# Spreading the queries over the edges: three bf16 products a chunk in place of one fp32 product

## The chip, the core and the metric

One core of a Trainium2 chip runs the whole program. Five engines work beside each other, each taking its own instructions in order: TensorE (PE; its weight loads are listed apart as PEld), VectorE (DVE), ScalarE (ACT), GpSimd (POOL) and SyncE (SP, which only issues transfers). The metric is the device time of one execution in microseconds (us), and lower is better. Three runs of the kernel before took 3375.17, 3377.44 and 3378.18 us; the median is 3377.44 us.

## The reference, cut to what matters

The program is a network of four graph layers with an expert layer behind each, over 3125 nodes of 256 features and 53125 edges. Only the first layer, the attention over the edges, is touched. There, each edge takes the dot product, per head, of its source's key and its destination's query:

```python
q = (nfeat @ Wq.T).reshape(n, HEADS, HEAD_DIM) / SCALING     # SCALING = 32 ** -0.5
k = (nfeat @ Wk.T).reshape(n, HEADS, HEAD_DIM)
v = (nfeat @ Wv.T).reshape(n, HEADS, HEAD_DIM)
attn = jnp.einsum('ehd,ehd->eh', k[src], q[dst])
attn = attn + attn_bias
m = jax.ops.segment_max(attn, dst, num_segments=n)
a = jnp.exp(attn - m[dst])
s = jax.ops.segment_sum(a, dst, num_segments=n)
a = a / s[dst]
out = jax.ops.segment_sum(v[src] * a[:, :, None], dst, num_segments=n)
return out.reshape(n, FEAT) @ Wo.T
```

The edges are sorted by destination. The change is in how `q[dst]` is made.

## The kernel before

The nodes are cut into 25 tiles of 125 (`P`, `T`). The edges that end in a tile lie in a window of 18 chunks (`WC`) of 128 edges. A chunk's rows of keys and values (2 KB an edge) are gathered from memory by POOL, one indirect transfer a chunk (`gathered`, L1656), six chunks to a tile `kv`, of which seven buffers exist.

`q[dst]` is a product with a one-hot matrix. The tile `oht` holds, for each of the 125 destinations (partitions) and each of the window's 2304 edges, whether the edge ends there. It arrives as a transfer of edge destinations to all partitions (`asked`, L1808), and a comparison with the partition's number on DVE turns it into ones and zeros in bf16, in place (`one_hot_turned`, L1834). Before the change ACT then casts it into fp32, in three tiles `oht_f` of six chunks (L1838). The queries of the tile (`queries`, L1825) are a product of the normalised rows with Wq on PE, scaled on ACT into an fp32 tile `q`.

`logits` (L1841) runs three times a tile, over six chunks each: for two chunks at a time PE multiplies `oht_f` with `q` into PSUM (L1849; the tile `qx`, two buffers), and DVE multiplies the keys by it in place (L1851). A reduction over each head's 32 features follows (L1852). `sums_of` (L1856) adds the edges' bias, takes the exponential on ACT, and sums it per destination by 18 small bf16 products (L1864), which DVE copies into `sums` (L1866). `weights_of` (L1868) makes the final weights, again with 18 small products, now with the bf16 `oht` (L1876). `weighted` (L1883) multiplies the values by them on DVE (L1886), casts the other one-hots into fp32 on ACT (`oh_f`, L1891), and adds up on PE (L1893; the tile `acc`). When `acc` has read a `kv` tile, POOL may fill it anew. `normed`, `normed_turned` and `projected` end the tile with an addition to `x` (L1917).

The loop at L1924 is a software pipeline: in iteration t the logits of tile t, the weights and sums of rows of tile t-1, and the one-hots and queries of tile t+1 are made; `beside` puts parts of the first expert layer in between (their products have the helper's line L266), and `windows.next()` parts of a preparation of a later stage, which sends a small table to memory and fetches it again (L2028 to L2040). A scheduler then orders each engine's instructions; SP's and POOL's queues keep the order in which they are built.

Of the kernel before, what the change touches and what calls it, by code (L numbers as in the profile page):

```python
# [10 lines left out]
F32 = mybir.dt.float32  # L11
F32R = mybir.dt.float32r
I32 = mybir.dt.int32
BF16 = mybir.dt.bfloat16
AF = mybir.ActivationFunctionType
# [7 lines left out]
N, D = 3125, 256  # L23
P, T = 125, 25
# [11 lines left out]
H, HD = 8, 32  # L36
# [12 lines left out]
WC, PC = 18, 6  # L49
# [21 lines left out]
def gnn_ffn_kernel(ctx: ExitStack, tc: tile.TileContext, a, out: bass.AP):  # L71
    nc = tc.nc
# [187 lines left out]
    def product(ps, terms, bias=None):  # L260

        last = len(terms) - 1
        if bias is not None:
            nc.tensor.matmul(ps, ones_h[:bias.shape[0], :ps.shape[0]], bias, start=True, stop=False)
        for i, (l, r) in enumerate(terms):
            nc.tensor.matmul(ps, l, r, start=(bias is None and i == 0), stop=(i == last))  # L266
# [1360 lines left out]
    def attention(windows, experts):  # L1627
# [11 lines left out]
        with ExitStack() as es:  # L1639
# [5 lines left out]
            sums = big.tile([P, T, H], F32, name="sums")  # L1645
# [10 lines left out]
            def gathered(at):  # L1656


                kv = rows_tile()
                for c in range(PC):  # L1660
                    got = nc.gpsimd.indirect_dma_start(  # L1661
                        out=kv[:, c, KO:], out_offset=None, in_=kv_d,
                        in_offset=bass.IndirectOffsetOnAxis(ap=src_i[:, at + c:at + c + 1], axis=0))
                    if len(under_way) > 4:
                        tc.add_manual_dep(got.ins, under_way[-5].ins.name, data_dep, reason="in turn")
                    under_way.append(got)
                nc.vector.memset(kv[:, :, KO - 1:KO], 1.0)
                return kv
# [3 lines left out]
            pool = setup.enter_context(tc.tile_pool(name="att_in", bufs=2, reuse_waits="tile"))  # L1672
# [128 lines left out]
            pool = es.enter_context(tc.tile_pool(name="att_s", bufs=2, reuse_waits="tile"))  # L1801
# [23 lines left out]
            def queries(s):  # L1825

                ps = psum.tile([P, D], F32, name="sm")
                product(ps, [(s.lt[:, k, :], wq[:, k, :]) for k in range(2)])
                s.q = pool.tile([P, D], F32, name="q")
                nc.scalar.activation(s.q, ps, AF.Copy, scale=float(HD) ** 0.5)  # L1830

            def one_hot_turned(s):
                v = s.oht.rearrange("d c e -> d (c e)")
                nc.vector.tensor_scalar(v, v, pcol[:P], None, ALU.is_equal)  # L1834
                s.oht_f = []
                for c0 in range(0, WC, PC):
                    s.oht_f.append(pool.tile([P, PC, 128], F32, name="oht_f", bufs=3))
                    nc.scalar.copy(s.oht_f[-1], s.oht[:, c0:c0 + PC, :])  # L1838
                s.l = pool.tile([128, WC, H], F32, name="l")

            def logits(s, p):  # L1841

                if p == len(s.kv):
                    s.kv.append(gathered(s.t * WC + p * PC))
                kv = s.kv[p]
                for c0 in range(0, PC, 2):
                    ps = psum.tile([128, 2, D], F32, name="qx", bufs=2)
                    for c in range(2):
                        nc.tensor.matmul(ps[:, c, :], s.oht_f[p][:, c0 + c, :], s.q, start=True, stop=True)  # L1849
                    k_ = kv[:, c0:c0 + 2, KO:VO]  # L1850
                    nc.vector.tensor_mul(k_, k_, ps)  # L1851
                nc.vector.tensor_reduce(  # L1852
                    s.l[:, p * PC:(p + 1) * PC, :],
                    kv[:, :, KO:VO].rearrange("p c (h d) -> p c h d", h=H), AX.X, ALU.add)

            def sums_of(s):  # L1856

                nc.vector.scalar_tensor_tensor(s.l, s.l, 640.0, s.eb.rearrange("p h c -> p c h"),
                                               ALU.min, ALU.add)
                el = pool.tile([128, WC, H], BF16, name="el")  # L1860
                nc.scalar.activation(el, s.l, AF.Exp, scale=1.0 / 8.0)
                ps = psum.tile([P, 512], F32, name="sm")
                for c in range(WC):
                    nc.tensor.matmul(ps[:, :H], s.oh[:, c, :], el[:, c, :], start=(c == 0),  # L1864
                                     stop=(c == WC - 1))
                nc.vector.tensor_copy(sums[:, s.t, :], ps[:, :H])  # L1866

            def weights_of(s):  # L1868

# [49 lines left out]
            now, before = asked(0), None  # L1919
            one_hot(now)  # L1920
            one_hot_turned(now)
            queries(now)
            more = experts()
            for t in range(T + 1):  # L1924
# [4 lines left out]
                if now:  # L1929
                    logits(now, 0)  # L1930
# [10 lines left out]
                if after:  # L1941
                    one_hot_turned(after)
                    queries(after)
                beside()
                if now:
                    logits(now, 1)
# [4 lines left out]
                if now:  # L1951
                    logits(now, 2)
# [3 lines left out]
                if now:  # L1956
                    sums_of(now)
# [572 lines left out]
```

## Time and profile before

The profiled execution took 3376.49 us; its span, from the first to the last instruction, is 3374.6 us. Shares of the span and counts, and the same for the stage of the attention, 121 to 870 us:

| engine | whole span, busy us | share | stage, busy us | share of 749 us |
|---|---|---|---|---|
| PE | 3116.4 | 92% | 692.8 | 92% |
| PEld | 2442.6 | 72% | 548.2 | 73% |
| DVE | 1704.7 | 51% | 571.7 | 76% |
| ACT | 1064.6 | 32% | 251.6 | 34% |
| POOL | 691.1 | 20% | 460.8 | 62% |

The costliest groups of the stage beside those that the change touches are, by line: L1893 on PE (the sums of rows, 213.9 us), L1852 on DVE (the reduction, 130.9 us), L1886 on DVE (the values times the weights, 127.6 us), and POOL's gathers (L1661, 451.7 us). The queries' own step on ACT, L1830, takes 9.4 us in 25 instructions, and the comparison L1834 on DVE 20.5 us in 25.

Two things help in reading these numbers. A matmul's end is modelled, and the next one starts before it, so a "mean ns of one" is longer than the time that it takes from PE; the distance between starts is that time. And a product of fp32 operands appears as two records.

### The profile page before, as it was taken

The page shows a single profiled execution, that of the slowest core. Times are in us where ns is not written, and L with a number is a line of the kernel's source. Part 1 is how long each engine was busy: PE and PEld are TensorE (multiplying, and loading weights), DVE is VectorE, ACT ScalarE, POOL GpSimd, SP SyncE. Part 2 cuts the span into 40 slices and gives each one's busy share as a digit, 9 for nine tenths or more (in the row PEclk, how much of TensorE's full clock was granted, in tenths as well). Part 3 has the DMA queues.
Part 4 walks back from the last instruction along what each step waited for, and adds up shares of the span by engine and source line. Part 5 has one row for each costly group of instructions (what it writes and reads, how often), then busy time and mean ns, then how long its engine had stood idle before and what let it go on. Part 6 is the DMA issues. An engine that isn't in the chain of part 4 may idle for free.

```text
span 3374.6 us, 43621 instructions
## 1 busy us (share of the span) xinstructions
PE 3116.4 (92%) x15687; PEld 2442.6 (72%) x15687; DVE 1704.7 (51%) x4763; ACT 1064.6 (32%) x2074; POOL 691.1 (20%) x639
## 2 busy tenths in 40 slices
PE   6698999999888999999996999979999999999898
PEld 2477777777677798898885888868755555579666
DVE  6587778777686434244673122166511111355662
ACT  1233333333355323232331222234323323332120
POOL 1676666655000000000234333200000000000000
PEclk9799999999899999999997999989999999999897
DMA  5876666655256634343445666564200000053001
GB/s 164 256 218 175 191 185 167 200 164 162 84 182 221 153 97 122 95 118 92 105 108 161 185 186 177 138 153 102 53 19 10 19 10 10 7 128 102 16 1 39
DMA packets 257578, 402.66 MB, mean 119 GB/s; under 512 B 42704, under 2 KB 202319, under 8 KB 257348
## 3 DMA queue, kind: packets, MB, share of 16 engines
q1 hardware_dynamic: 188465, 241.20, 25.6%
q0 software_dynamic: 54064, 141.25, 15.8%
q10 hardware_dynamic: 14819, 17.27, 2.0%
q8 instruction: 128, 2.10, 0.3%
q14 instruction: 102, 0.84, 0.1%
HBM read 328.87 MB, written 70.70 MB: 118 GB/s over the span
## 4 chain that ended last, share of the span: by engine, by line
PE 67%; DVE 5%; DMA 3%; issue 3%; ACT 2%; POOL 0%; SPq 0%; ACTq 0%; POOLq 0%; DVEq 0%
PE agg L2233 21%; PE po L266 19%; PE hid_ps L266 15%; PE tr L266 2%; PE row L266 1%; PE tok L1536 1%; PE acc L1893 1%; PE tr L2321 1%; PE tr L250 1%; DVE hr L282 1%; DMA kv<-kv_d,src_w 1%; PE qx L1849 1%; ACT h L1376 1%; DVE hc L282 0%; PE s L266 0%
## 5 line engine op out<-in xcount | busy, mean ns | idle before, releaser
L2233 PE MATMUL agg<-cnt_f,hp 125*128 125x500 f32 (+1 forms) x3500 | 733.7, 369 | 23.3 <-ACT hp L2174 22.9
L2233 PEld LDWEIGHTS agg<-cnt_f,hp 125*128 125x128 f32 x3500 | 635.9, 189 | 104.5 <-ACT hp L2174 24.0
L1661 POOL DMA_INDIRECT kv<-kv_d,src_w x450 | 467.4, 1039 | 233.5 <-issue 109.5
L2211 ACT CAST cnt_f<-blk 125x500 fp32r<-125x500 bf16 (+1 forms) x435 | 245.5, 565 | 519.5 <-PE agg L2233 489.7
L2211 DVE CAST cnt_f<-blk 125x500 fp32r<-125x500 bf16 (+1 forms) x440 | 184.9, 422 | 266.6 <-PE agg L2233 221.7
L1382 DVE SCALAR_TENSOR_TENSOR x<-po,gall,x 125x256 f32<-125x256 f32 x200 | 93.8, 484 | 417.5 <-PE po L266 416.9
L1376 ACT ACTIVATE h<-hid_ps,shift,scale 128x500 f32<-128x500 f32 (+1 forms) x224 | 161.7, 722 | 376.2 <-PE hid_ps L266 375.6
L1849 PE MATMUL qx<-q,oht_f 125*128 125x256 f32 x900 | 240.3, 399 | 14.6 <-DVE kv L1851 11.6
L1893 PE MATMUL acc<-kv,oh_f 128*125 128x265 f32 x900 | 219.2, 399 | 1.9 <-DVE kv L1886 1.9
L1849 PEld LDWEIGHTS qx<-q,oht_f 125*128 125x128 f32 x900 | 170.2, 197 | 50.3 <-DVE kv L1851 20.8
L266 PE MATMUL po<-wslot,h 128*125 128x256 f32 x800 | 203.0, 386 | 0.1
L1893 PEld LDWEIGHTS acc<-kv,oh_f 128*125 128x125 f32 x900 | 173.5, 194 | 37.0 <-DVE kv L1886 4.1
L266 PEld LDWEIGHTS po<-wslot,h 128*125 128x125 f32 x800 | 145.0, 187 | 75.2 <-ACT h L1376 27.0
L266 PE MATMUL hid_ps<-h,wslot 128*128 128x500 f32 (+1 forms) x448 | 193.6, 555 | 4.1 <-ACT h L1376 0.6
L1072 POOL DMA_INDIRECT xs_d<-r_l,pos x50 | 60.1, 1203 | 646.6 <-DVE r_l L1068 568.3
L266 PE MATMUL hid_ps<-xe,wslot 128*128 128x256 f32 x832 | 187.4, 383 | 1.8 <-DVE xe L1214 1.8
L1225 ACT ACTIVATE hid<-hid_ps,wslot 128x256 f32<-128x256 f32 x208 | 98.3, 474 | 287.2 <-PE hid_ps L266 287.2
L266 PE MATMUL hid_ps<-v_rows,wslot 128*128 128x500 f32 (+1 forms) x448 | 186.8, 537 | 0.0
L266 PE MATMUL po<-wslot,hid 128*128 128x256 f32 x832 | 184.5, 378 | 0.0
L266 PEld LDWEIGHTS hid_ps<-xe,wslot 128*128 128x128 f32 x832 | 150.8, 191 | 33.2 <-ACT hid L1225 3.6
L266 PEld LDWEIGHTS po<-wslot,hid 128*128 128x128 f32 x832 | 155.7, 189 | 21.8
L1851 DVE TENSOR_TENSOR kv<-kv,qx 128x512 f32<-128x512 f32 x225 | 150.7, 680 | 32.6 <-PE qx L1849 29.9
(509 smaller groups left out, 4535.4 us busy)
## 6 DMA issues: line engine op xcount, KB each, us to landing
wslot<-in_ex_W SPq DMA_DIRECT2D x52, 1024.0 KB
blk<-an_d SPq DMA_DIRECT2D x60, 546.9 KB
blk<-at_d SPq DMA_DIRECT2D x40, 546.9 KB
blk<-an_d SPq DMA_DIRECT2D x45, 410.2 KB
at_d<-ab SPq DMA_DIRECT2D x25, 683.6 KB
an_d<-an SPq DMA_DIRECT2D x25, 683.6 KB
oht<-turned_d SPq DMA_DIRECT2D x25, 504.0 KB
blk<-at_d SPq DMA_DIRECT2D x30, 410.2 KB
```

What stands on the lines that cost most here:

```text
L250: nc.tensor.transpose(ps[:, i * P:(i + 1) * P], src[:, i, k * 128:(k + 1) * 128], ident[:P, :P])
L266: nc.tensor.matmul(ps, l, r, start=(bias is None and i == 0), stop=(i == last))
L1072: st = nc.gpsimd.indirect_dma_start(out=xs_d, in_=l2[:, i, :].bitcast(I32), in_offset=None, out_offset=bass.IndirectOffsetOnAxis(ap=self.p ...
L1225: nc.scalar.activation(hid[:, m, :], ps[:, :BLK], AF.Gelu, bias=c[:, 4 + m:5 + m])
L1376: nc.scalar.activation(dst[:, m, :c], ps[:, :c], AF.Relu, bias=shift[:, l, col:col + 1], scale=scale[:, l, col:col + 1])
L1382: nc.vector.scalar_tensor_tensor(x[:, t0 + i, :], po, gating.all[:, t0 + i, e:e + 1], x[:, t0 + i, :], ALU.mult, ALU.add)
L1661: got = nc.gpsimd.indirect_dma_start(out=kv[:, c, KO:], out_offset=None, in_=kv_d, in_offset=bass.IndirectOffsetOnAxis(ap=src_i[:, at + c: ...
L1849: nc.tensor.matmul(ps[:, c, :], s.oht_f[p][:, c0 + c, :], s.q, start=True, stop=True)
L1851: nc.vector.tensor_mul(k_, k_, ps)
L1893: nc.tensor.matmul(s.acc[:, :D + H + 1], of[:, c, :], kv[:, c, AO:VO], start=(p == 0 and c == 0), stop=(p == 2 and c == PC - 1))
L2211: to(f[:, :n, :], part[0][:, :n, m % MB, :])
L2233: nc.tensor.matmul(ps[f][:, :c], hp[:, m, k, f * 128:(f + 1) * 128], got[:, :c], start=(m == 0 and k == 0), stop=(m == T - 1 and k == 1))
```

## The change

`queries` now splits the fp32 queries into three bf16 parts, whose sum carries them: the first part is the rounded query, the second the rounded rest, the third what is then left. `logits` multiplies each chunk's one-hots by the three parts in turn, adding up in PSUM, and takes the bf16 one-hots `oht` as the comparison leaves them. The casts into `oht_f` are gone, and so are its three buffers. The copy of the sums moves from DVE to ACT.

```diff
             def queries(s):
                 ps = psum.tile([P, D], F32, name="sm")
                 product(ps, [(s.lt[:, k, :], wq[:, k, :]) for k in range(2)])
-                s.q = pool.tile([P, D], F32, name="q")
-                nc.scalar.activation(s.q, ps, AF.Copy, scale=float(HD) ** 0.5)
+                s.q = pool.tile([P, 3, D], BF16, name="q_t")
+                q = pool.tile([P, D], F32, name="q", bufs=1)
+                nc.scalar.activation(q, ps, AF.Copy, scale=float(HD) ** 0.5)
+                nc.scalar.copy(s.q[:, 0, :], q)
+                nc.vector.tensor_sub(q, q, s.q[:, 0, :])
+                nc.scalar.copy(s.q[:, 1, :], q)
+                nc.vector.tensor_sub(s.q[:, 2, :], q, s.q[:, 1, :])

             def one_hot_turned(s):
                 v = s.oht.rearrange("d c e -> d (c e)")
                 nc.vector.tensor_scalar(v, v, pcol[:P], None, ALU.is_equal)
-                s.oht_f = []
-                for c0 in range(0, WC, PC):
-                    s.oht_f.append(pool.tile([P, PC, 128], F32, name="oht_f", bufs=3))
-                    nc.scalar.copy(s.oht_f[-1], s.oht[:, c0:c0 + PC, :])
                 s.l = pool.tile([128, WC, H], F32, name="l")
...
                     for c in range(2):
-                        nc.tensor.matmul(ps[:, c, :], s.oht_f[p][:, c0 + c, :], s.q, start=True, stop=True)
+                        for k in range(3):
+                            nc.tensor.matmul(ps[:, c, :], s.oht[:, p * PC + c0 + c, :], s.q[:, k, :],
+                                             start=(k == 0), stop=(k == 2))
...
-                nc.vector.tensor_copy(sums[:, s.t, :], ps[:, :H])
+                nc.scalar.copy(sums[:, s.t, :], ps[:, :H])
```

## The prediction

> **What bounds the kernel now.** I read the page first, then only the attention stage, 121 to 870 us: nothing else of the program is touched (the instructions after the loop stand in the same order in both programs).
>
> Groups of that stage by line, operation and shape (count | busy us, mean ns | idle before it and who ended it):
>
> ```profile
> L1849 PE MATMUL qx<-q,oht_f 125*128 125x256 f32 x900 | 240.3, 399 | 14.6 <-DVE kv L1851 11.6 <-DVE g_rank L716 1.3 <-DVE l L1879 0.5
> L1851 DVE TENSOR_TENSOR kv<-kv,qx 128x512 f32<-128x512 f32 x225 | 150.7, 680 | 32.6 <-PE qx L1849 29.9 <-DMA kv<-kv_d,src_w 1.8
> ...
> L1838 ACT CAST oht_f<-oht 125x768 f32<-125x768 bf16 x75 | 60.6, 829 | 59.6 <-PE qx L1849 26.9 <-DVE oht L1834 26.0 <-DVE kv L1667 5.9
> ```
>
> There are 18 chunks in each of 25 tiles, 450 products, but 900 records: one fp32 product is two passes over its 256 columns. ACT's casts cost 60.6 us, and ACT waits for others, not others for it: of the waits that end in a cast, PE's own are 2.1 us in all.
>
> The busy time of stretches (PE, PEld, DVE, ACT, POOL, each with its count; then the granted clock, the DMA share and GB/s) shows who sets the pace. I cut at each tile's last addition to x (L1917) and then over the stage:
>
> ```profile
> 642.00:676.40 34.40, 33.71 (x181) 26.72 (x180) 26.74 (x61) 11.00 (x23) 26.77 (x26) 1.00 0.77 219
> 676.40:700.90 24.50, 22.43 (x131) 17.74 (x129) 22.42 (x48) 9.99 (x20) 10.08 (x11) 1.00 0.48 139
> ...
> 270.20:308.40 38.20, 31.33 (x158) 23.83 (x157) 20.01 (x42) 11.19 (x23) 26.75 (x27) 0.87 0.80 189
> 121.00:870.00 749.00, 692.82 (x3734) 548.19 (x3735) 571.74 (x1155) 251.57 (x513) 460.79 (x441) 0.96 0.65 181
> ```
>
> Three kinds of tile. With the expert work beside it, a tile is PE's: 33.7 of 34.4 us busy, DVE waiting. Without, it is as much DVE's: 22.4 of 24.5 us on both. And some stand still for a transfer: in 270 to 308 PE is busy 31.3 of 38.2 us. Of the 24 tiles so cut, 13 have PE busy 95% or more; of the other 11, three early ones have POOL's gathers without a pause, about six stand for a transfer, the rest are DVE's.
>
> **PE, the main term.** The price of a product is the distance between starts, since ends are modelled. In the timeline (start, us, what):
>
> ```profile
> 617.82 1.89 PE L1849 MATMUL qx<-q,oht_f 125*128 125x256 f32 x8
> ...
> 625.03 0.59 PE L1876 MATMUL sm<-m,oht 125*128 125x8 bf16 x18
> ...
> 1056.94 0.56 PE L2121 MATMUL bt<-ident_h,ab 125*125 125x125 bf16 x7 [0.19 <-DVE an L2124]
> ...
> 3198.18 0.38 PE L264 MATMUL row<-bs,ones_h 128*125 128x512 bf16 x1
> 3198.40 1.02 PE L266 MATMUL row<-w_slices,lt 128*125 128x512 f32 x2
> ```
>
> An fp32 record of 256 columns takes (1.89 - 0.38)/7 = 216 ns, 0.38 being the modelled length of one, so a chunk takes 432 ns. No bf16 product of 256 columns is in the trace, but both neighbours are: 125 columns take (0.56 - 0.22)/6 = 56 ns, and 512 take 220 ns until the next start. On that line, 0.424 ns a column, 256 columns are 111.5 ns and three 335 ns: an estimate between two rows. Saved: 97 ns a chunk, 1.75 us a tile, 43.7 us over 25 tiles.
>
> Each of the three products has its own weight load (the new order shows a load ahead of each, 1350 against 900 records). Does it hide? The Trainium skill (TensorE: Matmul & The Clock Gate, "Back-to-back issue gap") speaks against this change: in a stream of load and product pairs both set the spacing, and it gives 81 ns where the streaming of 128 columns alone would give 56. By it each product costs some 25 ns more: 3 x 136.5 = 410 ns, and only 22 ns a chunk, 10 us in all, are saved. The row says otherwise: the 7 products of 125 columns above each have their own load of 125 columns and start every 56 ns; and 18 pairs with this very stationary operand, oht, take (0.59 - 0.17)/17 = 25 ns with 8 columns. A product of 111 ns has room for that. I take the row, load hidden, and keep the rule's 10 us as one end.
>
> Where does it arrive? In the 13 PE tiles at its full 1.75 us: -22.8 us. In the others PE isn't what ends the tile.
>
> **DVE.** Two subtractions a tile of 125x256 at 0.42 us, the row of L1917 (415 ns) and L242 (425 ns): 50 x 0.42 = +21.0 us. The output in bf16 isn't in the trace on this shape; between half that and that, I take that. The copy of the sums goes to ACT: 25 x 0.166 = -4.2 us, and so does its wait:
>
> ```profile
> L1866 DVE COPY sums<-sm 125x8 f32<-125x8 f32 x25 | 4.2, 166 | 16.9 <-PE sm L1864 16.9
> ```
>
> DVE stood 16.9 us there, with the multiplications of qx (L1851) behind it in its queue. L1872, which reads the sums, still needs them, but in the new order one or two other DVE instructions mostly stand ahead of it. Between 0 and 16.9 us come back; I take half, 8.5. DVE's net: 21.0 - 4.2 - 8.5 = +8 us, 0.33 us a tile; it counts in the 11 tiles that aren't PE's: +4 us.
>
> **The query chain and its waits.** The five steps, L1830 on ACT (0.38), copy (0.36 by L254, 365 ns), subtraction (0.42), copy, subtraction, take 2 us where one took 0.38. The queries are made one tile ahead, over 10 us before their first use, so PE doesn't wait. But each engine waits in the chain. The first subtraction stands on DVE in about half the tiles right after L1879, some 1.2 us after PE's 18 small products (L1876), when ACT's first copy is ready after about 1.6: 0.4 us of standing, with a multiplication behind it or the three long weightings (L1886) that PE's acc needs; 12 x 0.4 = +5 us at the most, and nothing where L1852 (1.75 us) is between. In five expert tiles it stands behind L1886 and ACT's second copy waits for it some 6 us; behind that only the last cast of oh (L1891) stands, for products that need the third L1886 anyhow. I take +2 us for all.
>
> **ACT.** Gone: 75 casts, 60.6 us, and the 59.6 us for which they held the queue waiting. Added: 50 copies of 0.36 us and 25 of 0.17: 22 us. ACT goes from 252 to 213 us of 749: worth PE's 2.1 us of waiting for a cast, -2 us. Where a wait goes, the next one is DVE's for oht.
>
> **SP, POOL, DMA.** No DMA issue is added or removed, and both queues keep their order. POOL's 450 gathers, 1.04 us plus 0.30 of issue each, are some 600 us of the stage, with 84.5 us of waiting for acc to free a buffer: enough cover for 24 us. The wait of L1834 for oht's transfer (24.1 us, 11 times) stays: the transfer is issued behind L1876, or behind the windows' round trip through memory (L2032), neither of which gets faster. That is why I give the standing tiles nothing.
>
> Sum against the profiled execution (span 3374.6 us, its own time 3376.5): -22.8 + 4 + 2 - 2 = -19; and a PE that comes earlier shortens some of DVE's 29.9 us of waiting for qx in the other tiles, of which I take a tenth, -3. That is -22 us: 3354.5 for that execution; the median of the three runs lies 0.9 us higher, so **3355 us**.
>
> **The rivals.**
> (a) The forecast, part of PE's saving arrives: 3342 to 3368. Chance 0.50.
> (b) All of it arrives, 43.7 us, as the stalls of DVE and ACT shrink too: 3377 - 44 = 3333. For it: PE is busy 92.5% of the stage, and 29.9 us of DVE's waits are for qx. Against: tiles with DVE at 92%. 0.20.
> (c) DVE, the gathers or oht's transfer take the place, and nothing to 9 us remains (the skill's spacing alone would leave 10 us of PE work): 3368 to 3384. 0.16.
> (d) Slower: the new loads aren't hidden. At 32 ns a product (97/3) the saving is gone. With the full 97 ns that a load of oht lasts (L1876's loads, mean) a chunk takes 3 x 208.5 = 626 ns, 87 us more, 3465; with half of it 3 x 160 = 480, 22 us more, 3399. For it: [...]none of this pair of shapes was seen. Against: the two rows above. 0.14.
> That the change does less than it says is out: the new order has the three products and no cast of oht.
>
> **Numbers.** A measurement of this kernel tells 0.2%, 6.8 us, from no change: faster is below 3370.7, slower above 3384.2. Faster: (a), (b) and a sliver of (c), 0.73; same 0.13; slower 0.14. The range reaches from just beyond (b) to within (c): 3330 to 3381.
>
> **What would show it.** Three bf16 products with starts 108 to 115 ns apart, and no cast of oht on ACT. PE's busy time in the stage near 650 of 725 us. Expert tiles near 32.6 us instead of 34.4, the tiles beside them as long as before. DVE's wait at the sums gone, a smaller one at the first subtraction. It is wrong if the starts lie 130 ns apart or more, if expert tiles keep their length, or if PE starts to wait for DVE at qx in them.

## The result, and the profile after

The changed kernel takes 3386.1 us in the median (3378.1 to 3396.3, 15 runs), the kernel before 3376.3 us on the same chip (3368.2 to 3382.8, 15 runs): a ratio of 1.0034 [1.0023, 1.0044]. It is slower by 10 us where 22 us less were forecast, and it lies above the predicted range. Its profiled execution has a span of 3382.4 us against 3374.6.

The first rows of the page after, its busy times (engine, us, share, instructions) and its group of the new product (count | busy, mean ns | idle before and its releaser):

```profile
PE 3097.9 (92%) x16137; PEld 2410.8 (71%) x16137; DVE 1718.4 (51%) x4788; ACT 1028.5 (30%) x2074; POOL 697.8 (21%) x639
...
L1851 PE MATMUL qx<-q_t,oht 125*128 125x256 bf16 x1350 | 202.0, 289 | 18.4 <-DVE kv L1854 14.2
```

PE has 18.5 us less to do than before (3116.4), and the span is 7.8 us longer. A PE that works less and waits more in a stage that it was thought to bound asks for the stage cut by tiles, as before. Columns: us, busy time and count of PE, PEld, DVE, ACT, POOL, then the granted clock (PEclk), the DMA share and GB/s:

```profile
274.20:318.10 43.90, 36.96 (x199) 27.18 (x199) 22.82 (x41) 8.73 (x22) 30.00 (x29) 0.88 0.76 180
502.40:527.50 25.10, 20.70 (x150) 16.49 (x150) 23.29 (x54) 8.67 (x20) 9.00 (x9) 1.00 0.43 123
...
650.10:682.20 32.10, 31.76 (x195) 24.30 (x195) 26.03 (x57) 9.14 (x22) 24.94 (x23) 1.00 0.75 214
682.20:711.30 29.10, 25.48 (x150) 19.65 (x150) 23.94 (x56) 9.04 (x21) 12.86 (x13) 0.82 0.50 144
121.00:877.00 756.00, 672.67 (x4167) 514.05 (x4167) 579.59 (x1175) 215.15 (x513) 467.98 (x442) 0.93 0.66 180
```

- The expert tile at 650 is 32.1 us long (34.4 before) and still PE's: this part came.
- The tile beside it, at 682, went from 24.5 to 29.1 us. The tile at 502 holds the same work, 150 records on PE, and takes 25.1. In one PE is busy 20.70 us, in the other 25.48, and the only column that tells them apart in kind is the clock: 1.00 and 0.82.
- The tile at 274, which stood for a transfer before (38.2 us), is now 43.9 us.
- The stage's granted clock fell from 0.96 to 0.93. Added up from the record of that clock, between the first small product of the weights (L1876, after the change L1879) and the last tile's end, called the loop from here on, PE is at half speed for 51 us before and for 89 us after.

The tiles at 650 and 682 us can be compared one by one, because each holds the spreading products of some 18 chunks in both kernels. Most other tiles cannot: the new order of the instructions moved work between them. In the expert tile at 214 us and the tile behind it stood 24 and 47 records of these products, two a chunk; now there are 55 and 53, three a chunk. So 12 and 24 chunks became 18 and 18, and in the tile without expert work PE, once busy 27.1 of 28.6 us, is now busy 24.2 of 28.2 (two lines of before, then two of after):

```profile
213.80:241.60 27.80, 27.60 (x149) 21.18 (x150) 18.85 (x38) 11.52 (x23) 21.09 (x21) 1.00 0.78 224
241.60:270.20 28.60, 27.12 (x157) 22.55 (x157) 25.50 (x53) 9.73 (x20) 20.15 (x19) 1.00 0.69 200
214.40:246.00 31.60, 31.31 (x192) 24.02 (x191) 22.39 (x36) 8.95 (x22) 24.90 (x23) 1.00 0.75 213
246.00:274.20 28.20, 24.22 (x150) 18.41 (x150) 24.04 (x56) 9.04 (x21) 21.11 (x18) 0.88 0.64 183
```

Added up by pairs of neighbours, the 24 tiles from the first tile's end to the last take 714.1 us before and 724.8 after. Seven of the 12 pairs have more half clock than before, 48 us together, and are 14.9 us longer; three have less, 10 us, and are 9.5 us shorter; two have as much and are 5.4 us longer.

Where do the 4.8 us of PE in the tile at 682 come from? The groups of PE in the two tiles, first the one at 502 and then the one at 682, both of the changed kernel:

```profile
L1896 PE MATMUL acc<-kv,oh_f 128*125 128x265 f32 x36 | 8.3, 389 | 0.0
L1851 PE MATMUL qx<-q_t,oht 125*128 125x256 bf16 x54 | 7.1, 272 | 0.3
...
L1896 PE MATMUL acc<-kv,oh_f 128*125 128x265 f32 x36 | 11.2, 483 | 0.1
L1851 PE MATMUL qx<-q_t,oht 125*128 125x256 bf16 x53 | 8.3, 298 | 1.5 <-DVE kv L1854 1.3
```

The 36 records of the sums of rows, a line that the change does not touch, take 2.9 us more. The same tile in steps of 3.4 us (columns as above):

```profile
685.00:688.40 3.40, 3.40 (x31) 2.67 (x30) 3.09 (x7) 0.00 (x0) 2.54 (x3) 0.52 0.79 233
688.40:691.80 3.40, 2.37 (x19) 1.71 (x18) 1.99 (x6) 2.82 (x5) 0.95 (x1) 1.00 1.00 288
691.80:695.20 3.40, 2.16 (x16) 1.45 (x15) 3.40 (x5) 2.17 (x7) 0.00 (x0) 0.98 0.41 124
695.20:698.70 3.50, 3.36 (x10) 2.73 (x11) 3.50 (x3) 0.00 (x0) 0.00 (x0) 0.50 0.00 0
698.70:702.10 3.40, 3.40 (x9) 2.57 (x9) 1.55 (x4) 0.31 (x1) 0.07 (x1) 0.53 0.00 0
702.10:705.50 3.40, 3.40 (x17) 2.86 (x16) 2.86 (x5) 1.40 (x3) 2.79 (x3) 1.00 0.28 77
```

From 691.8 to 695.2 PE is busy 2.16 of 3.4 us. Then the clock is 0.50 for two steps, although PE works almost without a pause in both, and these two steps hold the sums of rows. The timeline of PE (start, us, what, idle before it) shows what the pauses are:

```profile
690.83 0.81 PE L1851 MATMUL qx<-q_t,oht 125*128 125x256 bf16 x6 [0.87 <-DVE kv L1854]
692.12 0.49 PE L1851 MATMUL qx<-q_t,oht 125*128 125x256 bf16 x3 [0.48 <-DVE kv L1854]
...
693.67 0.43 PE L250 MATMUL tr<-ident,ln 125*128 125x125 f32 x2 [0.46 <-ACT lt L254]
694.56 1.40 PE L266 MATMUL tr<-wslot,lt 128*125 128x4 f32 x8 [0.46 <-ACT lt L254]
696.09 11.16 PE L1896 MATMUL acc<-kv,oh_f 128*125 128x265 f32 x36
```

None is over 0.9 us here. PE now finishes its spreading products sooner than DVE multiplies them (L1854, 682 ns for a pair of chunks), waits for the buffer, works 0.3 us and waits again, for DVE or for ACT's copies of the turned rows (`lt`). In the same place before, the fp32 products filled most of this time: the waits there are 0.24 and 0.27 us, the clock stays at 1.00, and the sums of rows take 8.29 us:

```profile
683.22 1.97 PE L1849 MATMUL qx<-q,oht_f 125*128 125x256 f32 x8 [0.24 <-DVE l L1879]
686.11 1.13 PE L1849 MATMUL qx<-q,oht_f 125*128 125x256 f32 x4 [0.27 <-DVE kv L1851]
688.95 8.29 PE L1893 MATMUL acc<-kv,oh_f 128*125 128x265 f32 x36
```

### The profile page after: what moved, and what is told of

Its sections match the earlier page's. It is cut to its first block, busy times and chain, and to the rows that moved or that the text cites. A ratio compares the mean times of both kernels' runs of the same rounds, so it can differ in the third digit from the quotient of the medians.

```text
span 3382.4 us, 44414 instructions
## 1 busy us (share of the span) xinstructions
PE 3097.9 (92%) x16137; PEld 2410.8 (71%) x16137; DVE 1718.4 (51%) x4788; ACT 1028.5 (30%) x2074; POOL 697.8 (21%) x639
## 3 DMA queue, kind: packets, MB, share of 16 engines
q8 instruction: 132, 2.16, 0.3%
## 4 chain that ended last, share of the span: by engine, by line
PE 77%; DVE 8%; DMA 7%; issue 4%; ACT 2%; POOL 1%; SPq 0%; ACTq 0%; DVEq 0%; POOLq 0%
PE agg L2236 21%; PE po L266 19%; PE hid_ps L266 15%; PE acc L1896 5%; PE tr L266 4%; DMA kv<-kv_d,src_w 2%; PE qx L1851 1%; PE row L266 1%; PE tok L1536 1%; POOL kv L1661 1%; DVE kv L1854 1%; DMA ptr_d<-ptr 1%; PE tr L250 1%; PE sm L266 1%; PE tr L2324 1%
## 5 line engine op out<-in xcount | busy, mean ns | idle before, releaser
L2236 PEld LDWEIGHTS agg<-cnt_f,hp 125*128 125x128 f32 x3500 | 636.6, 189 | 103.6 <-ACT hp L2177 23.5
L1851 PE MATMUL qx<-q_t,oht 125*128 125x256 bf16 x1350 | 202.0, 289 | 18.4 <-DVE kv L1854 14.2
L1851 PEld LDWEIGHTS <-oht 125*128 125x128 bf16 x1350 | 138.5, 104 | 61.8 <-issue 25.0
L1854 DVE TENSOR_TENSOR kv<-kv,qx 128x512 f32<-128x512 f32 x225 | 150.2, 682 | 29.3 <-PE qx L1851 28.6
```

The lines of the kernel that those rows point to most:

```text
L1851: nc.tensor.matmul(ps[:, c, :], s.oht[:, p * PC + c0 + c, :], s.q[:, k, :], start=(k == 0), stop=(k == 2))
L2236: nc.tensor.matmul(ps[f][:, :c], hp[:, m, k, f * 128:(f + 1) * 128], got[:, :c], start=(m == 0 and k == 0), stop=(m == T - 1 and k == 1))
```

## The experiments

Two theories were set against each other, with a third added as the runs came in. **K, the clock**: with less work, PE pauses in the tiles without expert work, is granted half clock for it, and pays the saving back in the work that follows. **C, the chain**: the five steps of the queries, on ACT and DVE, hold up work queued behind them. **O, the order**: any change of the products makes the scheduler order the instructions anew, and that alone moves the time. In the expectations of i1 and i2 the letter C stands for the clock.

Ratios are against the kernel before, on the same chip each time. The kernels named f and g ran on chips like the first one, where it takes 3368 to 3371 us; those named e, h and i on chips where the very same program takes 3672 to 3681 us; in the kernels profiled there the 300 us more lie within the attention stage. Ratios are therefore compared only between chips of one sort, and the times expected of e1 to e4, which are those of the first sort, are judged by f1 to f4.

### A fourth product, of zeros, in all tiles

```diff
-                        for k in range(3):
+                        for k in range(4):
-                            nc.tensor.matmul(..., s.q[:, k, :],
+                            nc.tensor.matmul(..., s.q[:, k, :] if k < 3 else q_zero,
```

> A fourth bf16 product a chunk, of a tile of zeros, is added to the changed kernel: PE's work for a chunk is 436 ns (4 x 109), as before the change (432), all else is as changed. Theory K (the PE time set free turns into gaps, the granted clock drops to half for more of the stage, 101 us against 62, and takes the saving back): the half clock's share falls back to about 62 us of the stage and the time stays where it is or falls, 3376 to 3387. Theory C (the added chain of casts and subtractions between ACT and DVE lengthens the tiles that DVE bounds, and PE's saving does count in the others): the 13 tiles that PE bounds get 1.96 us longer each, +25 us, about 3411.

> The kernel with a fourth product, of zeros, again, on a chip on which the kernel before takes about 3376 if that is to be had. Theory K (freed PE time turns into gaps and half clock): ratio to the kernel before 0.999 to 1.004, half clock in the stage near 60 us. Theory C (chain and hand-overs; PE's time counts in the PE tiles): 1.008 to 1.012.

Measured: f1 3385.0 us, 1.0036 [1.0024, 1.0048]; e1 3706.5 us, 1.0069 [1.0056, 1.0082]. At 109 ns each the 450 added products are 49 us of PE, and they cost nothing against the changed kernel's 1.0034, as K expected (0.999 to 1.004; C 1.008 to 1.012). In f1 seven of the tiles without expert work are at 23.4 to 24 us where the changed kernel had 25 to 29, and half clock in the loop falls from 89 to 51 us; five expert tiles are at 35.3 to 35.8 us where it had 31.7 to 32.1. The two cancel. So more work on PE shortens some tiles.

### No chain, and the sums copied on DVE again

```diff
-                nc.scalar.activation(q, ps, AF.Copy, scale=float(HD) ** 0.5)
-                nc.scalar.copy(s.q[:, 0, :], q)
-                nc.vector.tensor_sub(q, q, s.q[:, 0, :])
-                nc.scalar.copy(s.q[:, 1, :], q)
-                nc.vector.tensor_sub(s.q[:, 2, :], q, s.q[:, 1, :])
+                nc.scalar.activation(s.q[:, 0, :], ps, AF.Copy, scale=float(HD) ** 0.5)
...
-                nc.scalar.copy(sums[:, s.t, :], ps[:, :H])
+                nc.vector.tensor_copy(sums[:, s.t, :], ps[:, :H])
```

The first edit is that of e3 and f2, which multiply by the one part three times and so leave out the second and third parts of the queries; the second edit, alone, is that of e4 and f4.

> No split: ACT writes one bf16 part from PSUM, and all three products take this part (the queries lose their second and third part). PE's work is as changed, two casts on ACT and two subtractions on DVE a tile are gone, and the hand-overs between them. Theory C: the chain's 21 us of DVE and its waits (12 us of DVE for ACT) come back, 15 to 30 us, 3356 to 3371, below the kernel before. Theory K: within 6 us of the changed kernel, 3380 to 3392, with the half clock as long.

> The kernel without the split (one bf16 part, taken three times, no chain) again. Theory C: ratio to the kernel before 0.993 to 0.998. Theory K: 1.001 to 1.005, the half clock as long as in the changed kernel (about 90 us of the loop).

> The copy of the sums goes back to DVE, all else as changed. By the prediction's term it costs 4.2 us of work and half of 16.9 us of waiting in tiles that DVE bounds: +5 to +10, about 3393. Theory K: no difference beyond 4 us. A third theory (the copy on ACT makes ACT wait for PE, 29.7 us, with the chain's casts queued behind it): 5 to 10 us shorter, about 3378.

> The changed kernel with the copy of the sums back on DVE again. The prediction's term: 5 to 10 us more than the changed kernel, ratio to the kernel before 1.005 to 1.006. If the copy on ACT hurts the chain behind it: 1.000 to 1.002.

Measured: f2 3369.0 us, 0.9991 [0.9979, 1.0002]; e3 3702.3, 1.0052 [1.0038, 1.0067]; f4 3384.3, 1.0038 [1.0027, 1.0050]; e4 3706.1, 1.0075 [1.0062, 1.0088].

Where the sums are copied makes no difference (1.0038 and 1.0034), so neither the cost nor the gain that was expected of it came. Without the chain the kernel is some 14 us faster, between what C (0.993 to 0.998) and K (1.001 to 1.005) expected; e3 against e4 gives 8 us on the other sort of chips. Half clock lasts about as long as in the changed kernel (85 and 89 us), so these 14 us are not the clock's. The tile that began at 274 us gives 10.2 of them (43.8 to 33.6), the fifteenth 3.2. In the changed kernel's timeline that tile reads (SPq is SP issuing a transfer):

```profile
285.81 1.70 SPq L108 DMA_DIRECT2D oht<-turned_d  x1
...
295.67 0.82 DVE L1839 TENSOR_SCALAR oht<-oht,pcol 125x2304 bf16<-125x2304 bf16 x1 [7.86 <-DMA oht<-turned_d]
296.40 0.42 DVE L1833 TENSOR_TENSOR q<-q,q_t 125x256 f32<-125x256 f32 x1
296.86 0.41 ACT L1834 CAST q_t<-q 125x256 bf16<-125x256 f32 x1 [7.05 <-DVE q L1833]
298.66 0.47 ACT L781 ACTIVATE e<-tr,wslot 128x250 f32<-128x250 f32 x1
299.18 1.09 PE L266 MATMUL pair<-e,wslot 128*64 128x250 f32 x2 [2.71 <-ACT e L781]
```

DVE's comparison waits 7.86 us for the one-hots' transfer, the first subtraction stands behind it, ACT's second copy waits 7.05 us for that, an activation of the expert work stands behind the copy, and PE waits 2.71 us for it. Nothing in this chain needs the one-hots; only the queues tie it to them. Without the chain ACT has no copy to wait with: f2's comparison waits 5.21 us, and its tile is 33.6 us.

### Two parts instead of three

```diff
-                s.q = pool.tile([P, 3, D], BF16, name="q_t")
+                s.q = pool.tile([P, 2, D], BF16, name="q_t")
+                nc.scalar.activation(s.q[:, 0, :], ps, AF.Copy, scale=float(HD) ** 0.5)
+                nc.vector.scalar_tensor_tensor(s.q[:, 1, :], ps, float(HD) ** 0.5, s.q[:, 0, :],
+                                               ALU.mult, ALU.subtract)
...
-                        for k in range(3):
+                        for k in range(2):
```

This is f3, which leaves out the third part of the queries; e2 leaves out only the third product and keeps the chain as it is.

> The third product is left out (the queries lose their third part; it is still computed): PE does 218 ns a chunk. Theory K: PE has more gaps, more than 101 us of the stage at half clock, and the time stays within 6 us of the changed kernel's 3386. Theory C: another 1.96 us off each of 13 tiles, about 3361.

> Two parts only, made in two steps: ACT writes the first from PSUM in bf16, DVE the second as the rest (the queries lose their third part). PE does 218 ns a chunk, DVE has one operation where the change has two, no tile waits twice for the other engine. Theory C: DVE +0.3 us and PE -3.8 us a tile against before: ratio 0.985 to 0.993. Theory K: PE has still more gaps, the clock is low for more than 90 us, and the ratio is 0.998 to 1.003.

Measured: e2 3686.6 us, 1.0015 [1.0006, 1.0024]; f3 3358.7 us, 0.9955 [0.9940, 0.9970]. A third less of the products, 49 us of PE, and a shorter chain bring 27 us against the changed kernel (0.0079 x 3371). PE's busy time in the loop falls by 28 us, not by 49, and half clock lasts 135 us there instead of 89. The time lies between C's 0.985 to 0.993 and K's 0.998 to 1.003. On the other sort of chips, dropping the third product gives 0.6% (1.0015 against 1.0075 [1.0062, 1.0088] of e4, which has three and copies the sums on DVE).

### Zero products only in the tiles without expert work

```diff
-                        for k in range(3):
+                        terms = 3 + (1 if s.t % 2 else 0)
+                        for k in range(terms):
```

That is g1, the changed kernel with 18 products of zeros more in every second tile. g4 and g2 do it to the two parts of f3, with one and with two products of zeros (both leave out the third part). i1 does it to the kernel before, and i2 adds only 9 a tile, on the first chunk of each pair.

> The changed kernel with the fourth product, of zeros, only in the odd tiles, whose logits fall into the tiles without expert work (those that DVE bounds). Theory K (the half clock in these tiles eats the saving): they take 23.4 to 24 us instead of 28 to 29, the others stay at 32.1, the half clock falls to about 60 us, and the ratio to the kernel before is 0.990 to 0.996. If PE's clock in these tiles is only a symptom of waiting (theory C): no tile gets shorter, ratio 1.003 to 1.006.

> The two-part kernel in two steps (0.9955 of before) with two more products of zeros in the odd tiles. Theory K: tiles with expert work near 28 to 30 us as in the two-part kernel, the others 23.4 to 24: ratio 0.985 to 0.990. Theory C: the added 98 us x 12/25 of PE work lie under DVE and change nothing: 0.995 to 0.997.

> The two-part kernel with one more product of zeros in the odd tiles. Theory K: between the two-part kernel and the one with two of zeros, 0.988 to 0.994, with the half clock between theirs. Theory C: 0.995 to 0.997.

> The kernel before, with one bf16 product of zeros a chunk added in every second tile (s.t odd: the tiles with no expert work beside them); nothing is taken out. Theory C (a PE with short gaps in the light tiles drops to half clock, and more work there keeps it up): half clock in the attention loop falls from 51 us to under 30, the light tiles take about 23.5 to 25 us and the kernel gains 5 to 15 us, ratio 0.995 to 0.999, although PE has 24 us more to do. Rival O (in the changed kernel it was only the new order of instructions that the zeros brought): added work gains nothing here, ratio 1.000 to 1.006.

> The changed kernel with half of the filler: a product of zeros on the first chunk of each pair only, in every second tile, 9 a tile instead of 18. Theory C: time goes with the half clock left in the loop; between 45 and 90 us of it, and a time between the changed kernel's 1.0034 and 0.9975, near 1.000. Rival O: each order of instructions has its own time, and the half clock and the light tiles' length need not go together: a light tile at full clock may be 28 us or more.

| without the zeros | ratio | with them | ratio | difference, us | half clock in the loop, us |
|---|---|---|---|---|---|
| the changed kernel | 1.0034 [1.0023, 1.0044] | g1 | 0.9975 [0.9964, 0.9986] | -20 | 89 to 44 |
| f3, two parts | 0.9955 [0.9940, 0.9970] | g4, one | 0.9943 [0.9930, 0.9957] | -4 | 135 to 79 |
| f3, two parts | 0.9955 [0.9940, 0.9970] | g2, two | 0.9914 [0.9900, 0.9928] | -14 | 135 to 51 |
| h2 (below) | 1.0081 [1.0066, 1.0097] | h3 | 1.0043 [1.0031, 1.0056] | -14 | 412 to 362 |
| the kernel before | 1 | i1 | 0.9942 [0.9921, 0.9962] | -21 | not known, 332 |
| the changed kernel, h1 | 1.009, a single run | i2 | 0.9999 [0.9984, 1.0014] | -34 | 455 to 383 |

(The differences are those of the ratios times the time of the kernel before on that chip.) Work that computes nothing makes four different kernels faster, on two sorts of chips; g4's 4 us alone are within the intervals, and h1's row rests on a single run. g1 gained less than K's 0.990 to 0.996, g2 (0.985 to 0.990) too, and g4 came in at the edge of its range. The tile of g1 that answers to the one at 682 us, cut in the same way, and its sums of rows in the timeline:

```profile
667.70:692.10 24.40, 22.50 (x163) 18.33 (x162) 22.38 (x51) 8.68 (x20) 11.21 (x12) 0.93 0.52 156
```

```profile
679.41 8.21 PE L1899 MATMUL acc<-kv,oh_f 128*125 128x265 f32 x36
```

There are 13 more records in it than in the changed kernel's tile and 3 us less of PE's time, and the tile is 4.7 us shorter. Six other tiles of g1 are at 23.4 to 23.5 us, with no half clock. That is 1.7 us less than the 25.1 that such a tile takes at full clock in the changed kernel, so the clock is not all that changed there; the expert tile ahead of this one takes 34.0 us in g1 where it took 32.1. By pairs of tiles, the seven that lose half clock against the changed kernel (57 us) are 29.8 us shorter, and the three that gain some (13 us) are 3.7 us longer.

i1 was expected at 0.995 to 0.999 and gained more; its other figures, 30 us of half clock and tiles of 24 us, were worked out for the first sort of chip and do not hold on the one that it ran on (332 us, and 30 to 46 us a tile). i2 came in where the clock put it (near 1.000); its tiles on that chip do not decide between K and O.

### The chain on the kernel before, and the queries ahead of the comparison

g3 adds to the kernel before two casts on ACT and two subtractions on DVE a tile, whose results nothing uses:

```diff
                 nc.scalar.activation(s.q, ps, AF.Copy, scale=float(HD) ** 0.5)
+                parts = pool.tile([P, 3, D], BF16, name="q_t", bufs=1)
+                nc.scalar.copy(parts[:, 0, :], s.q)
+                nc.vector.tensor_sub(parts[:, 2, :], s.q, parts[:, 0, :])
+                nc.scalar.copy(parts[:, 1, :], parts[:, 2, :])
+                nc.vector.tensor_sub(parts[:, 2, :], s.q, parts[:, 1, :])
```

h2 is the changed kernel with `queries(after)` ahead of `one_hot_turned(after)`, to take the subtraction from behind the comparison; h3 is g1 and h4 is g2 with the same exchange; h1 is the changed kernel beside them. It was to set K against O tile by tile, and could not, since it ran on the other sort of chip.

> The kernel before with the chain of two casts on ACT and two subtractions on DVE a tile added, its result not used; products and one-hots as before. PE is as busy as before, so theory K gives the clock nothing to do: half clock near 51 us. Theory C: the chain by itself costs what it costs in the changed kernel (1.0034 against 0.9991 without it), 10 to 18 us: ratio 1.003 to 1.005. By the prediction (DVE's work only, in 11 tiles, and 2 us of waits): 1.002 to 1.003.

> The changed kernel once more, for a second profile of the same order of instructions. Theory K: the tiles without expert work that hold no half clock take 25 us, each 3.4 us of it adds about 1.4 us, whichever tiles it falls into this time; a tile that changes its share changes its length. Theory O (the order of instructions sets these lengths, the clock follows): each tile takes what it took, 28 to 29 us at the second, fourth, sixth, eighth and eighteenth, 25 at the twelfth and fourteenth, whatever the clock.

> The changed kernel with queries(after) built ahead of one_hot_turned(after), so that the chain's first subtraction no longer stands on DVE behind the comparison that waits for oht's transfer, and ACT's second copy not behind it. If the chain costs by standing behind that transfer (14 us between the changed kernel and the one without a chain, 10 of them in the fifth tile): ratio 0.999 to 1.001, the fifth tile near 34 us instead of 44. If it costs by its work: 1.003 to 1.004, the fifth tile as long.

> The same order of the calls, and the fourth product of zeros in the odd tiles (0.9975 without the order). If the two causes add up: 0.993 to 0.996. If they are one: 0.997 to 0.999.

> The fastest kernel so far (two parts in two steps, two products of zeros in the odd tiles, 0.9914) with the same order of the calls. Its one subtraction, too, then stands ahead of the comparison: 0.988 to 0.991 if that standing still costs there, else 0.991 to 0.992.

Measured: g3 3363.1 us, 0.9984 [0.9977, 0.9991]; h1 3711.5 (a single run, 3676.8 before); h2 3704.5, 1.0081 [1.0066, 1.0097]; h3 3690.2, 1.0043 [1.0031, 1.0056]; h4 3645.1, 0.9916 [0.9903, 0.9929].

The chain's 21 us on DVE and 20 on ACT cost the kernel before nothing, where 1.002 to 1.005 were expected, so C holds only together with the rest: where the order puts the chain behind a comparison that waits for its transfer, and expert work behind the chain. In g3 the fifth tile takes 28.1 us, 10 us less than in the kernel before itself, which nothing in the four added instructions explains but a new order. Half clock in the loop is 23 us, where K expected the 51 us of before: the order moves the clock, too. The exchange in h2 gained no more than a single run can tell, and h2 and h3 lie above all that was expected of them. Those were the other sort of chips, where half clock (412 us) and waits of another kind cover 14 us, so on the first sort its worth is open. h4 stands where g2 stood (0.9916 and 0.9914): what the two parts with zeros gain, they gain on both sorts.

## Why the prediction was wrong

- **The price on PE: right.** Starts of the new products lie 109 ns apart (111.5 estimated), each with its own load: the six from 690.83 us on take 0.81 us, of which the last is 0.27. By the Trainium skill's spacing (TensorE: Matmul & The Clock Gate, "Back-to-back issue gap") the estimate was 136.5. Rival (d), loads that do not hide, is out, although its sign came true.
- **"In the 13 PE tiles at its full 1.75 us", -22.8 us: right in the tile, wrong in the sum.** The expert tile at 650 us is 2.4 us shorter. But the 13 tiles were counted in the old order, which gave some tiles without expert work 24 chunks; in the changed kernel PE is busy 95% or more in 8 tiles only.
- **Expert tiles shorter, "the tiles beside them as long as before": this step failed.** It left the clock at what the rows before showed, 1.00 in those tiles, and so gave the others nothing, neither gain nor loss. The clock did not stay. The tile at 682 us went from 24.5 to 29.1 us, and at 502 us, where the clock stays at 1.00, such a tile takes 25.1. With 10.2 us at half clock that is 0.4 us for each, an estimate from two tiles; the 38 us more of half clock in the loop make 15 us at this rate, and the 44 us fewer in g1 18 us, where 20 were measured.
- **The query chain and its waits, "+2 us for all": the place was right, the size was not.** The first subtraction waits 12.1 us for ACT. ACT's second copy waits 15.0 us, as forecast in kind, but 13.4 of them in two tiles, at 274 and 587 us. But "behind that only the last cast of oh (L1891) stands" is not so in the tile at 274 us, where an activation that PE needs stands there. The runs put some 14 us on the chain (f2), against 2.

```profile
L1833 DVE TENSOR_TENSOR q<-q,q_t 125x256 f32<-125x256 f32 x25 | 10.6, 423 | 12.2 <-ACT q_t L1832 12.1
L1834 ACT CAST q_t<-q 125x256 bf16<-125x256 f32 x25 | 9.9, 397 | 15.0 <-DVE q L1833 15.0
...
L1869 ACT COPY sums<-sm 125x8 f32<-125x8 f32 x25 | 4.1, 165 | 29.7 <-PE sm L1867 29.7
```

- **DVE's +8 us, of which half the wait at the sums returns: not borne out.** The subtractions cost what was said (423 and 418 ns), and the wait went to ACT, as the groups of the stage after show (29.7 us on L1869). With the copy back on DVE the time is the same.
- **ACT's -2 us and the -3 us for DVE's waits on qx: not tested**, and too small to be seen in a total that missed the forecast by 32 us.
- **"I give the standing tiles nothing"** was too kind: the one at 274 us lost 5.7 us, which are part of what the chain cost.

Together: -22 forecast, +10 measured. 20 us come back with the zero products and 14 without the chain, which is about the missing 32 if the two add up. That they do is not shown: each of these runs also has a new order, and a kernel with three full parts, the zeros and no such queueing was not run.

The Trainium skill (TensorE: Matmul & The Clock Gate, "The HAM clock gate") says that the clock is either half or full and follows PE's activity in windows of about 3.4 us. The trace agrees with the values and with the length: every stretch of half clock in the loop is a multiple of 3.4 us. The page's short form of the rule ("HAM oscillation — how this bites in real kernels"), no idle time on PE above about 3.4 us, would have let this kernel pass: the longest single wait in the tile at 682 us is 1.38 us. The pauses add up to 1.2 of 3.4 us in the step ahead of the slow one; but the step before that had 1.0 us and the clock stayed. It also stayed where PE did still less in two such steps, so no limit can be read here:

```profile
609.80:613.20 3.40, 1.91 (x10) 1.07 (x10) 1.20 (x8) 1.30 (x3) 2.79 (x3) 1.00 0.23 43
613.20:616.60 3.40, 1.96 (x9) 1.58 (x10) 3.25 (x9) 0.00 (x0) 2.48 (x4) 1.00 0.68 204
616.60:620.00 3.40, 3.40 (x24) 2.86 (x23) 1.90 (x4) 0.37 (x1) 2.49 (x4) 1.00 0.80 217
```

**What stays open.** Each kernel with zeros also has another order of instructions on PE, DVE and ACT, so O is not excluded, and how much of the 10 us is the order's stays open. Against it: the same sign in all six comparisons, less half clock in the five where both kernels were profiled, and within one run of the changed kernel tiles of equal work that differ by their clock. For it: g3, where a new order with nothing taken from PE goes with 28 us less half clock and 5 us less time, the chunks that moved between tiles, and the 23.4 us tiles of g1. And half clock is not the whole of it: f3 has more of it than the changed kernel and is faster, with a third less of the products and a shorter chain; f4 has 75 us of it instead of 89 and takes the same time.

## What to carry to other kernels

Before taking work from PE in a stage where it alternates with another engine, look at the tiles where it is not the bound: if its pauses there grow (here to a third of 3.4 us), the next stretch may run at half clock, and the saving is paid back by work that was not touched. Check, too, which tiles PE still fills in the new order before counting a saving in them. Cost a step of a chain by what is queued behind its wait on each engine, tile by tile, for the tile that stands for a transfer above all. And try the cheap counter-test: g1, the changed kernel with products of zeros where PE pauses, keeps all three parts and is faster than both kernels (0.9975 [0.9964, 0.9986] of the kernel before); g2, with two parts, is the fastest run here (0.9914 [0.9900, 0.9928]), if the queries can do without their third part.

## What the runs showed of the hardware

- Half clock costs where it falls, not where it is earned: the 36 records of the sums of rows took 8.3 us at full clock and 11.2 us where half clock followed a step in which PE had stood for 1.2 us.
- Adding PE work shortened a kernel in which PE is the busiest engine: 24 us of zero products took 21 us off the kernel before (i1, 0.9942 [0.9921, 0.9962]; PE busy 88% of the span with them).
- The same program took 3672 to 3681 us on some chips and 3368 to 3376 on others. In h1 on such a chip the waits of PE begin with these (waited for: us in total, times, longest us); "issue" is time for which the profile shows no cause:

```profile
PE qx L1851 <- DVE kv L1854: 96.7, 41, 7.6
PE tr L266 <- issue: 56.2, 19, 6.9
```

What follows the loop took 2490 us there and 2489 here. Half clock lasted 332 to 485 us in the loop of all the kernels profiled on those chips. Why was not tried.
